# Moving a projection, two prefetches and an image load to other units of a software-pipelined Mamba block

## The chip, the cores and the metric

The kernel runs on one core of one Trainium2 chip. The metric is the device time in microseconds of one launch. The kernel before takes 27343.99 us, the median of three runs from 27331.65 to 27346.93 us. A further execution was recorded by the profiler; its own time is 27302.98 us, and the span that the profile shows is 27301.2 us.

The engines have the names that the profile uses. PE is the matrix engine, and PEld its weight load. DVE is the vector engine, ACT the scalar engine (activation functions and copies), POOL the GpSimd engine. SP only issues DMA transfers here. Each engine carries out its own list of instructions in order and waits on semaphores for the others.

## The reference

The input is a batch of 8 images with 64 channels and 128 x 128 pixels, all in float32. The first layer reads every image as sequences of 128 pixels, once along its rows and once along its columns. Each sequence goes through a small Mamba block forwards and backwards, the results are averaged, normalised in four groups of channels, passed through SiLU and added to the image:

```
x, z  = split(in_w @ seq);  x = silu(causal_conv4(x) + conv_b)
dt, B, C = split(xp_w @ x); delta = softplus(dt_w @ dt + dt_b)
h_t = exp(delta_t * A) * h_{t-1} + (delta_t * x_t) * B_t      # 128 channels, 16 states
y_t = sum_states(h_t * C_t) + D * x_t;  out = out_w @ (y * silu(z))
```

The second layer is a residual block: its weights are drawn from a small parameter vector, and it computes 3 x 3 convolution, batch norm, ReLU, 3 x 3 convolution, batch norm, addition of its input, ReLU.

## The kernel before

**Chunks.** An image is cut into 32 chunks of four rows (o = 0, "row chunks") and then 32 chunks of four columns (o = 1, "column chunks"), each chunk 512 pixels. With 8 images that is 512 chunks. `PER` = 64 is the number of chunks of an image; below, a chunk is named by its number within the image, 0 to 63. For a row chunk the input is read straight from the resident image `xt` in SBUF; for a column chunk ACT first gathers its pixels into `xc` (L253).

**Units.** A chunk is worked through in 16 units, r = 0 to 15. A unit is one pair of 32-channel groups, four of the 16 states and one direction, laid out as 128 partitions x 1024 elements. The steps of a unit are:

- `decay` (L361, L364): ACT writes exp(A * delta) into one of two PSUM tiles, `dA0` for even units and `dA1` for odd ones. So decay of unit s+1 has to wait until the scan of unit s-1 has read that tile.
- `b_rows` (L353): PE spreads the B rows of two units into the PSUM tile `pb`.
- `drive` (L373): DVE multiplies `du` (delta times x) by `pb` into `s`. In the units 2, 5, 9, 12 and 15 (`GPS`) POOL does this instead, from a tile `bt` that a DMA has spread.
- `scan` (L381 forwards, L383 backwards): DVE runs the recurrence in place in `s`.
- `weigh` (L388): POOL multiplies `s` by the C rows.
- `add_up` (L404): PE folds two finished units into the output tile `yp`, four units later.

**The next chunk and the last one.** While the units of chunk n run, `prepare` takes one step per unit for chunk n+1: convolution and input projection into `cp` (L235 or L241, units 1 to 4), SiLU (unit 5), `dp` (L273, unit 6), `bp` and `bc` (L278, L283, unit 7), softplus (unit 8), `du` and `dl` and their stores to DRAM (L300, L302, L295, unit 9), the replicated loads of `dl` and `du` (L324, units 10 to 13), and `zp` with its copy `sz` (L315, unit 13). The chunk before is finished: DVE gates `yp` with `sz` in unit 3 (L411), and `emit` then projects it. PE multiplies by out_w into the PSUM tile `op` (L417); in a column chunk it also adds the row result, read transposed through an identity matmul (L422). ACT copies `op` into the image result `xp` (L430 for rows, L435 twice for columns). For a column chunk DVE then takes statistics of what was written (`bn_stats`, L439). In the kernel before these are units 12, 13 and 14.

**Shared buffers.** The PSUM tiles `cp`, `dp`, `op`, `cps` (first convolution of the second layer) and `gps` (normalisation) use one buffer, tag "pt". `pb`, `bp` and `zp` use another, tag "b". A tile can be written only when the readers of the tile before it are done. The image `xt`, the image result `xp` and two `strip` tiles exist once.

**Work per image.** When the last column chunk of an image has been projected, in chunk 0 of the next image, the statistics are combined (`normalize`). In the chunks 1 to 16, units 5 and 7, ACT normalises a part of `xp`, POOL adds the input and the sum is stored to DRAM as `x1`. The first convolution (`conv1`) reads `x1` back in strips: `strip_of` issues two or more DMAs per strip, and the matmuls (L494) start in unit 14 of chunk 6, three steps of two matmuls and a copy per chunk. Its first two strips are issued by the first call of the generator, `next(conv3, None)`. The next image is loaded into `xt` in chunk 62.

**The order** is written out by hand: the main loop runs over the units and calls these steps, and every engine gets its instructions in that order. All the DMAs named here are issued by SP, in one list with the waits that the program put in front of each of them; an issue that waits holds up the ones behind it. The rest of the kernel, the second convolution and the last pass, follows the loop and is not touched.

Of the kernel before, what the change touches and what calls it, by code (L numbers as in the profile page):

```python
# [17 lines left out]
W = 128  # L18
HH = W // 2
# [13 lines left out]
def tile_mamba2d_then_resblock(ctx: ExitStack, tc: tile.TileContext, x, par, gn, p_w, o_w, new_p, bn, cst, out):  # L33
    nc = tc.nc
    B = x.shape[0]
# [30 lines left out]
    with tc.tile_pool(name="prep", bufs=2) as prep, tc.tile_pool(name="prep_ps", bufs=2, space=PSUM) as prep_ps:  # L66
# [4 lines left out]
        for o, p in enumerate(par):  # L71
# [10 lines left out]
            for hf in range(2):  # L82
                h = slice(hf * C, (hf + 1) * C)
# [72 lines left out]
        for k, w in enumerate((w1, w2s)):  # L156
            nc.vector.memset(w, 0.0)
            for blk in range(2):
                for e in range(2):
                    for m in range(2):  # L160
                        kh = 2 * blk - e - m + 1
                        if 0 <= kh < 3:
                            nc.sync.dma_start(
                                out=w[e * C : (e + 1) * C, blk, :, m * C : (m + 1) * C],
                                in_=wacc[k * C : (k + 1) * C, 3 * kh : 3 * kh + 3, :],
# [37 lines left out]
    with ExitStack() as st:  # L203
# [9 lines left out]
        xt = big.tile([P, HH, W], F32, name="xt")  # L213
# [6 lines left out]
        zeros = big.tile([P, 2, SEQ], F32, name="zeros")  # L220
        nc.vector.memset(zeros, 0.0)

        def load_image(b):
            xb = x[b].rearrange("p (h w) -> p h w", w=W)
            RB = HH // 8
            for k in range(8):
                nc.sync.dma_start(out=xt[:, k * RB : (k + 1) * RB, :], in_=xb[:, k * RB : (k + 1) * RB, :])

        def project(ps, lhsT, g, s, start, stop):

# [103 lines left out]
        def c_rows(g, r):  # L334

            half, ng, d = where(r)
            t = rep.tile([P, N], F32, name="c", bufs=5)
            src = g["bd"][NS + 4 * ng : NS + 4 * ng + 4, d, :]
            nc.sync.dma_start(out=t, in_=src.partition_broadcast(32))
            g["c", ng, d] = t  # L340

        def b_tile(g, r):

            half, ng, d = where(r)
            t = rep.tile([P, N], F32, name="bt", bufs=3)
            nc.sync.dma_start(out=t, in_=g["bd"][4 * ng : 4 * ng + 4, d, :].partition_broadcast(32))
            g["bt", r] = t

        def b_rows(g, r):

            half, ng, d = where(r)
            pb = psa.tile([P, N], F32, name="pb", tag="b")
            nc.tensor.matmul(pb, wt[g["o"]]["wb"][:, P * ng : P * (ng + 1)], g["u"][:, d, :], start=True, stop=True)  # L353
            g["pb"] = pb

        def decay(g, r):

            half, ng, d = where(r)
            dA = g["dA", r] = psa.tile([P, 2, SEQ, W], F32, name=f"dA{half}")
            t, edge = (slice(1, W), 0) if d == 0 else (slice(0, W - 1), W - 1)  # L360
            nc.scalar.copy(dA[:, :, :, edge], zeros)  # L361
            dl = g["dl", half, d].rearrange("p q (s t) -> p q s t", t=W)
            for j in range(2):
                nc.scalar.activation(  # L364
                    dA[:, j, :, t], dl[:, j, :, t], AF.Exp, scale=wt[g["o"]]["A"][:, 2 * half + j, ng : ng + 1]
                )

        def drive(g, r):

            half, ng, d = where(r)  # L370
            s = unit.tile([P, 2, N], F32, name="s")
            engine, b = (nc.gpsimd, g.pop(("bt", r))) if r in GPS else (nc.vector, g["pb"])
            engine.tensor_mul(s, g["du", half, d], b.unsqueeze(1).to_broadcast([P, 2, N]))  # L373
            g["s", r] = s
# [10 lines left out]
        def weigh(g, r):  # L385
            half, ng, d = where(r)
            s, c = g["s", r], g["c", ng, d]
            nc.gpsimd.tensor_mul(s, s, c.unsqueeze(1).to_broadcast([P, 2, N]))  # L388
# [123 lines left out]
        PER = 2 * NCH  # L512
# [2 lines left out]


        PREP = range(14)
        OUT = 12
        NORM = (5, 7)
        CONV = (14, 15, 0, 1, 2)  # L520
        gs = [dict(b=b, o=o, i=i) for b in range(B) for o in range(2) for i in range(NCH)]
        total = UN * len(gs)
        stats = {}
        pieces, norm, conv3, output = (iter(()) for _ in range(4))

        def at(s):
            return gs[s // UN], s % UN

        def fetch(s):

            for k in range(10):
                r = (s + k) % UN
                if 0 <= s + k < total and r in GPS and k == {GPS[0]: 9, GPS[1]: 4}.get(r, 7):
                    b_tile(*at(s + k))
                if 0 <= s + k < total and r % 2 == 0 and k == {0: 7, 4: 4}.get(r, 5):
                    c_rows(*at(s + k))

        def ahead(r):

            return 2 if r == GPS[0] else 3  # L540

        with tc.manual_schedule():
            load_image(0)
            for _ in prepare(gs[0], None):
                pass
            for s in range(-9, 0):
                fetch(s)
            decay(*at(0))
            b_rows(*at(0))
            drive(*at(0))  # L550
            for s in range(total + UN):
                n, r = divmod(s, UN)
                live = n < len(gs)
                prev = gs[n - 1] if n else None
                if r == 0:
                    for _ in pieces:
                        pass
                    pieces = prepare(gs[n + 1], gs[n]) if n + 1 < len(gs) else iter(())
                if s + 1 < total:
                    decay(*at(s + 1))  # L560
                    if (s + 1) % UN not in GPS:
                        drive(*at(s + 1))
                for k in (2, 3):
                    if s + k < total and (s + k) % UN in GPS and ahead((s + k) % UN) == k:
                        drive(*at(s + k))
                if live:
                    scan(*at(s))
                    weigh(*at(s))
                if r == LAG - 1 and prev:
                    gate(prev)  # L570
                if s == total - 1:
                    nc.scalar.activation(gs[n]["sz"], gs[n]["sz"], AF.Silu)
                if s % 2 == 0 and s + 2 < total:
                    b_rows(*at(s + 2))
                if r in CONV and n % PER > 6 or r >= CONV[0] and n % PER == 6:
                    next(conv3, None)
                if r in PREP:
                    next(pieces, None)
                if r == LAG and live:
                    skip(gs[n])  # L580
                if s % 2 == 0 and LAG <= s < total + LAG:
                    add_up(*at(s - LAG))
                if r in NORM and n % PER:
                    next(norm, None)
                fetch(s)
                if r == OUT and prev:
                    if n % PER == 6:
                        next(conv3, None)
                    output = emit(prev)
                    next(output)  # L590
                elif r == OUT + 1:
                    next(output, None)
                elif r == OUT + 2:
                    next(output, None)
                    if n % PER == 0 and prev:
                        for _ in conv3:
                            pass
                        norm = normalize(prev["b"], stats.pop(prev["b"]))
                        next(norm)
                        conv3 = conv1(prev["b"])  # L600
                elif r == 8 and live and n % PER == PER - 2 and gs[n]["b"] + 1 < B:
                    load_image(gs[n]["b"] + 1)

            for _ in range(2 * 5):
                next(norm)
            next(conv3)
            for _ in range(NT):
                for _ in range(2):
                    next(norm, None)
                for _ in range(5):  # L610
                    next(conv3)


    with ExitStack() as st:
# [15 lines left out]
        mean, r = pooled(small, [pps[:, 0:1], pps[:, 1:2]], mv, bmat, "bn1")  # L630
# [8 lines left out]
        st2 = small.tile([P, B, NT, 6], F32, name="st2")  # L639
        RB = HH // 4  # L640
        for b in range(B):
            xp = xps[b % 2]
            cb = c1_d[b].rearrange("p (h w) -> p h w", w=W)
            for k in range(0, HH + 1, RB):
                ct = stage.tile([P, RB, W], F32, name="ct")
                for e in range(2):
                    es = slice(e * C, (e + 1) * C)
                    lo, hi = max(k, e), min(k + RB, HH + e)
                    if lo < hi:
# [5 lines left out]
                if 0 < k < HH:  # L655
                    nc.scalar.activation(xp[:, k : k + RB, 1 : W + 1], ct, AF.Relu, bias=t, scale=s)
            c2v = c2_d[b].rearrange("(v c) (j e w) -> v c j e w", c=C, e=2, w=W)
            for k in range(0, NT, 2):
                ps = psw.tile([P, 2, N], F32, name="cps")
                for j in range(2):  # L660
                    for kw in range(3):
                        for blk in range(2):
                            r = SEQ * (k + j) + blk
# [10 lines left out]
                for e in range(2):  # L674
                    nc.sync.dma_start(
                        out=c2v[hf, :, j0 : j0 + 2 * SEQ, e, :],
                        in_=cs[e * C : (e + 1) * C].rearrange("p (j w) -> p j w", w=W),
# [4 lines left out]
        mean, r = pooled(small, [pps[:, 2:3], pps[:, 3:4]], mv2, bmat, "bn2")  # L682
# [72 lines left out]
```

## Time and profile before

| | value |
|---|---|
| median of three runs | 27343.99 us |
| profiled execution, its own time | 27302.98 us |
| its span | 27301.2 us |
| DVE busy | 25670.1 us, 94% |
| POOL busy | 25128.9 us, 92% |
| PE busy | 19712.4 us, 72% |
| ACT busy | 18444.1 us, 68% |
| one DVE scan (L381, L383) | 2.28 us, 8192 of them |
| one DVE drive (L373) | 1.20 us, 5632 of them |
| one POOL operation (L388, L373) | 2.36 and 2.37 us, 8192 and 2560 of them |
| granted PE clock, mean | 0.857 of full speed |
| DMA traffic | 4871.19 MB, 178 GB/s |

In a line of the waits view stand the engine and line that waited, what it waited for, the sum in us, how often, and the longest. In a line of the timeline stand the start and the duration in us, the engine, the line of the kernel, the operation, the tiles that it writes and reads, the shape, and how many instructions were merged; in brackets is the idle time of the engine before it and what ended it. A line of the windows view gives a stretch in us from the start of the span, its length, the busy time of the five engines in it with the number of instructions, the granted PE clock, the share of DMA time and the rate.

Where several semaphores are waited for, the profile names the one that came last by its records; an engine that had been done long before is then not the cause.

### The profile page before, as it was taken

To read this page: it belongs to the slowest core of one execution; us is meant where nothing else is said; L and a number is where in the kernel's file an instruction comes from. 1 tells how busy PE (TensorE), PEld (TensorE's weight loads), DVE (VectorE), ACT (ScalarE), POOL (GpSimd) and SP (SyncE) were. 2 spreads that over 40 slices of the span, in tenths; PEclk is the share of its full clock that TensorE was granted. 3 is DMA by queue.
4 is the path that set the end of the run, shared out by engine and by line. 5 is a ranking of instruction groups with operands and counts; after the bars stand their busy time and mean duration, and the time that the engine had idled before them with its cause. 6 is when DMAs were issued, how large, how long until landed. Compare 5 with 4: busy or idle time off the path is not lost.

```text
span 27301.2 us, 235600 instructions
## 1 busy us (share of the span) xinstructions
PE 19712.4 (72%) x65580; PEld 6768.1 (25%) x65580; DVE 25670.1 (94%) x15633; ACT 18444.1 (68%) x31150; POOL 25128.9 (92%) x10916
## 2 busy tenths in 40 slices
PE   6777777777777777777677777777777777777776
PEld 1222222222222222222222222222222222222232
DVE  8999999999999999999999999999999999999942
ACT  5776667676677766767667666676676766667632
POOL 7999999999999999999999999999999999999930
PEclk8888888888888889888888888888888888888888
DMA  5555555555555455555555555555555555555545
GB/s 180 177 173 172 181 186 183 175 170 181 194 179 173 170 184 194 179 171 170 186 193 176 172 174 186 188 176 173 175 189 184 173 175 178 190 181 171 177 139 188
DMA packets 2165563, 4871.19 MB, mean 178 GB/s; under 512 B 265856, under 2 KB 413456, under 8 KB 2148368
## 3 DMA queue, kind: packets, MB, share of 16 engines
q1 hardware_dynamic: 2143648, 4754.51, 51.6%
q10 hardware_dynamic: 15984, 68.06, 0.9%
q0 software_dynamic: 4608, 33.56, 0.3%
q8 instruction: 517, 8.47, 0.1%
q14 instruction: 806, 6.60, 0.1%
HBM read 4115.52 MB, written 738.98 MB: 178 GB/s over the span
## 4 chain that ended last, share of the span: by engine, by line
DVE 35%; PE 25%; issue 21%; ACT 9%; DMA 7%; SPq 2%; POOL 1%; DVEq 0%; POOLq 0%; ACTq 0%
DVE s L373 14%; DVE s L383 10%; DVE s L381 8%; PE pb L353 7%; PE yp L404 6%; DMA du<-dd 5%; ACT dA L364 4%; PE cps L664 2%; PE dp L273 2%; DVE du L300 2%; PE cp L241 2%; PE op L417 1%; DVE y L411 1%; PE op L422 1%; PE bp L278 1%
## 5 line engine op out<-in xcount | busy, mean ns | idle before, releaser
L388 POOL TENSOR_TENSOR s<-s,c 128x1024 f32<-128x1024 f32 x8192 | 19135.7, 2363 | 887.2 <-DVE s L383 596.3
L364 ACT ACTIVATE dA<-dl,A 128x508 f32<-128x508 f32 x16384 | 11275.4, 688 | 534.8 <-DMA dl<-dd 18.0
L353 PE MATMUL pb<-u,wb 128*128 128x512 f32 x8192 | 5589.3, 770 | 7026.0 <-DVE s L373 6298.3
L383 DVE TENSOR_TENSOR_SCAN s<-dA,s 128x1024 f32<-128x1024 f32 x4096 | 9301.2, 2281 | 51.6 <-ACT dA L364 43.1
L381 DVE TENSOR_TENSOR_SCAN s<-dA,s 128x1024 f32<-128x1024 f32 x4096 | 9296.8, 2280 | 0.0
L373 DVE TENSOR_TENSOR s<-du,pb 128x1024 f32<-128x1024 f32 x5632 | 6776.9, 1203 | 269.9 <-PE pb L353 156.5
L373 POOL TENSOR_TENSOR s<-du,bt 128x1024 f32<-128x1024 f32 x2560 | 6066.2, 2370 | 207.3 <-DMA bt<-bd 154.9
L404 PE MATMUL yp<-s,fold 128*32 128x512 f32 x32768 | 5386.0, 736 | 2.8 <-POOL s L388 2.8
L361 ACT COPY dA<-zeros 128x8 f32<-128x8 f32 x8192 | 1375.8, 168 | 5700.8 <-DVE s L383 3245.0
L353 PEld LDWEIGHTS pb<-u,wb 128*128 128x128 f32 x8192 | 1523.5, 223 | 10331.1 <-DVE s L373 5159.3
L241 PE MATMUL cp<-xc,wc 128*128 128x256 f32 (+3 forms) x8192 | 2190.9, 414 | 0.0
L235 PE MATMUL cp<-xt,wc 128*128 128x512 f32 (+3 forms) x4096 | 2033.1, 620 | 127.3 <-DMA xt<-x_h 75.9
L241 PEld LDWEIGHTS cp<-xc,wc 128*128 128x128 f32 x8192 | 1676.7, 211 | 1074.4 <-issue 461.2
L404 PEld LDWEIGHTS yp<-s,fold 128*32 128x32 f32 x32768 | 699.9, 117 | 3863.7 <-POOL s L388 2139.0
L364 ACT ACT_TABLE_LOAD x1030 | 1321.5, 1283 | 26.5 <-DMA dl<-dd 8.4
L315 ACT COPY sz<-zp 128x512 f32<-128x512 f32 x512 | 300.1, 586 | 1331.1 <-PE zp L241 852.1
L235 PEld LDWEIGHTS cp<-xt,wc 128*128 128x128 f32 x4096 | 770.6, 199 | 1433.5 <-issue 1071.4
L273 PE MATMUL dp<-u,wd 128*128 128x512 f32 x2048 | 978.6, 601 | 1.2 <-ACT u L266 1.2
L394 PE MATMUL yp<-u,dg 128*128 128x512 f32 x2048 | 961.9, 592 | 1.0 <-DVE y L411 1.0
L693 POOL DMA_DIRECT2D out<-cc x32 | 17.2, 537 | 968.7 <-ACT cc L692 968.7
L494 PE MATMUL cps<-strip,w 128*128 128x512 f32 x1536 | 750.5, 615 | 104.1 <-DMA strip<-x_d 88.1
L417 PE MATMUL op<-y,wo 128*128 128x512 f32 x1024 | 720.4, 792 | 0.8 <-DVE y L411 0.8
(109 smaller groups left out, 10513.4 us busy)
## 6 DMA issues: line engine op xcount, KB each, us to landing
dl<-dd SPq DMA_DIRECT2D x2048, 512.0 KB
du<-dd SPq DMA_DIRECT2D x2048, 512.0 KB
c<-bd SPq DMA_DIRECT2D x4096, 256.0 KB
bt<-bd SPq DMA_DIRECT2D x2560, 256.0 KB
dd<-du SPq DMA_DIRECT2D x2048, 128.0 KB
dd<-dl SPq DMA_DIRECT2D x2048, 128.0 KB
bd<-bc SPq DMA_DIRECT2D x512, 128.0 KB
c_d<-cs SPq DMA_DIRECT2D x256, 256.0 KB
```

Of the source, the lines that this page charges most:

```text
L235: nc.tensor.matmul(ps[:, :, lo:hi], lhsT[hf], xt[:, r : r + SEQ, lo - s : hi - s], start=start, stop=stop)
L241: nc.tensor.matmul(ps[:, :, lo:hi], lhsT[hf], g["xc"][:, :, lo - s - hf * HH : hi - s - hf * HH], start=start and hf == 0, stop=stop and h ...
L273: nc.tensor.matmul(dp[:, d, :], w["wd"], u[:, d, :], start=True, stop=True)
L353: nc.tensor.matmul(pb, wt[g["o"]]["wb"][:, P * ng : P * (ng + 1)], g["u"][:, d, :], start=True, stop=True)
L361: nc.scalar.copy(dA[:, :, :, edge], zeros)
L364: nc.scalar.activation(dA[:, j, :, t], dl[:, j, :, t], AF.Exp, scale=wt[g["o"]]["A"][:, 2 * half + j, ng : ng + 1])
L373: engine.tensor_mul(s, g["du", half, d], b.unsqueeze(1).to_broadcast([P, 2, N]))
L381: nc.vector.tensor_tensor_scan(s, a, s, 0.0, ALU.mult, ALU.add)
L383: nc.vector.tensor_tensor_scan(s[:, ::-1], a[:, ::-1], s[:, ::-1], 0.0, ALU.mult, ALU.add)
L388: nc.gpsimd.tensor_mul(s, s, c.unsqueeze(1).to_broadcast([P, 2, N]))
L404: nc.tensor.matmul(g["yp"][32 * q : 32 * (q + 1), :], fold, s[:, j, :], start=False, stop=r == UN - 2, skip_group_check=True,)
L417: nc.tensor.matmul(op, w["wo"].rearrange("p h c -> p (h c)"), g["y"], start=True, stop=o == 0)
```

## The change

`OUT` goes from 12 to 10: the projection of the chunk before is issued in unit 10, its copies in unit 11, and for a column chunk its statistics in unit 12. In the first chunk of an image the statistics of the image before and the start of its normalisation move with them. The first call of `conv3`, which issues an image's first two strips, goes from unit 12 to unit 2 of chunk 6. `load_image` issues one eighth of an image per call instead of all eight; it is called in the units 2, 4, 6 and 8 of the chunks 62 and 63 instead of once in unit 8 of chunk 62. The first image is still loaded at once ahead of the loop. The number of instructions and of DMAs and their sizes stay as they were.

```diff
-        def load_image(b):
-            xb = x[b].rearrange("p (h w) -> p h w", w=W)
-            RB = HH // 8
-            for k in range(8):
-                nc.sync.dma_start(out=xt[:, k * RB : (k + 1) * RB, :], in_=xb[:, k * RB : (k + 1) * RB, :])
+        def load_image(b, k):
+
+            rows = slice(k * (HH // 8), (k + 1) * (HH // 8))
+            nc.sync.dma_start(out=xt[:, rows, :], in_=x[b].rearrange("p (h w) -> p h w", w=W)[:, rows, :])
...
-        OUT = 12
+        OUT = 10
         NORM = (5, 7)
         CONV = (14, 15, 0, 1, 2)
+        LOAD = (2, 4, 6, 8)
...
-            load_image(0)
+            for k in range(8):
+                load_image(0, k)
...
                 fetch(s)
+                if r == CONV[-1] and n % PER == 6:
+                    next(conv3, None)
+                if r in LOAD and live and n % PER >= PER - 2 and gs[n]["b"] + 1 < B:
+                    load_image(gs[n]["b"] + 1, LOAD.index(r) + 4 * (n % 2))
                 if r == OUT and prev:
-                    if n % PER == 6:
-                        next(conv3, None)
                     output = emit(prev)
                     next(output)
...
-                elif r == 8 and live and n % PER == PER - 2 and gs[n]["b"] + 1 < B:
-                    load_image(gs[n]["b"] + 1)
```

## The prediction

> **What bounds the kernel now.** I read the page's busy shares first, then the table of waits, then four consecutive chunks cut out by windows, then the timeline of one chunk.
>
> ```profile
> PE 19712.4 (72%) x65580; PEld 6768.1 (25%) x65580; DVE 25670.1 (94%) x15633; ACT 18444.1 (68%) x31150; POOL 25128.9 (92%) x10916
> ```
>
> DVE is busy 94% of the span, POOL 92%, and the slices show that most of what DVE lacks lies in the last two of forty, where the second convolution runs. In the main loop DVE is the bound with POOL close behind. A saving must therefore be DVE idle time in the loop:
>
> ```profile
> DVE gst L439 <- ACT xp L435: 329.3, 191, 5.1
> ...
> DVE s L373 <- PE pb L353: 156.5, 237, 8.0
> ...
> DVE s L373 <- DMA du<-dd: 103.7, 93, 11.6
> ...
> PE cps L494 <- DMA strip<-x_d: 88.1, 13, 28.5
> ```
>
> (Columns: total, times, longest, us.) The statistics of a column chunk wait for ACT's copies 191 times; about 590 us of idle on DVE is what any reordering here can reach. Four column chunks, from first scan to first scan:
>
> ```profile
> 5697.27:5749.86 52.59, 38.95 (x132) 14.97 (x132) 49.78 (x32) 35.85 (x62) 48.73 (x22) 0.81 0.52 179
> 5749.86:5799.36 49.50, 34.99 (x132) 13.73 (x132) 49.49 (x31) 35.86 (x62) 48.73 (x22) 0.89 0.46 159
> 5799.36:5850.80 51.44, 37.81 (x132) 14.53 (x132) 49.78 (x31) 35.85 (x62) 48.78 (x22) 0.83 0.51 173
> 5850.80:5902.07 51.27, 37.63 (x132) 14.47 (x132) 49.78 (x31) 35.85 (x62) 48.79 (x22) 0.83 0.53 177
> ```
>
> (Length, then busy PE, PEld, DVE, ACT, POOL, granted clock.) The second has DVE busy 49.49 of 49.50: this is a column chunk's floor. The others lose 1.8 to 3.1 us, with a lower PE clock. The mean of the 248 ordinary column chunks is 51.15. The end of the fourth on PE, then on DVE:
>
> ```profile
> 5882.77 2.08 PE L353 MATMUL pb<-u,wb 128*128 128x512 f32 x2 [5.70 <-DVE s L373]
> 5884.77 1.93 PE L404 MATMUL yp<-s,fold 128*32 128x512 f32 x8
> 5888.26 2.08 PE L353 MATMUL pb<-u,wb 128*128 128x512 f32 x2 [1.56 <-DVE s L373]
> 5890.27 1.52 PE L404 MATMUL yp<-s,fold 128*32 128x512 f32 x8
> 5891.71 1.12 PE L417 MATMUL op<-y,wo 128*128 128x512 f32 x2
> 5892.68 1.88 PE L422 MATMUL op<-xp,ident 128*128 128x512 f32 x2
> 5894.37 1.04 PE L241 MATMUL zp<-xc,wz 128*128 128x256 f32 x4
> ```
> ```profile
> 5888.12 2.29 DVE L381 TENSOR_TENSOR_SCAN s<-dA,s 128x1024 f32<-128x1024 f32 x1
> ...
> 5893.71 2.27 DVE L383 TENSOR_TENSOR_SCAN s<-dA,s 128x1024 f32<-128x1024 f32 x1
> 5897.18 0.43 DVE L439 BATCH_NORM_STATS2 gst<-xp 128x6 f32<-128x256 f32 x1 [1.20 <-ACT xp L435]
> ```
>
> PE does add-up (8,9), the projection, zp in one row; ACT copies sz, then xp twice; DVE has finished scan 14 at 5895.98 and waits until 5897.18. The first pb takes 2.08 us after 5.70 us of idle and 1.12 later: PE is slow after idling.
>
> [...] its clock changes on a 3.413 us grid, no slow window less than 0.81 busy was followed by a fast one, and the four chunks above sum to 204.80 us, 60 windows: the chunks have locked to that grid. [...] the xp copy behind sz (5895.94 after 5895.45, both long after op ended) agrees. [...] SP's timeline of a load chunk agrees:
>
> ```profile
> 6542.43 6.16 SPq L227 DMA_DIRECT2D xt<-x_h  x8
> 6549.48 4.02 SPq L295 DMA_DIRECT2D dd<-du  x4
> 6554.47 4.42 SPq L295 DMA_DIRECT2D dd<-dl  x4
> ```
>
> In the chunk before, each group of four stores took 1.73 and 1.81.
>
> **Projection at unit 10, copies 11, statistics 12.** Nothing is added or removed: the two column matmuls (one in row chunks), two copies (one) and one statistics instruction move two units up, and no DMA with them. Call 5882.77 zero. DVE ends scan 12 at +7.64, and the statistics now stand behind it. PE reaches the projection behind add-up (6,7): +2.00 plus 1.87 slow is +3.88. Its wait on the dp buffer is met (du and dl are read by then). Slow, op takes 1.87 and ident 1.72, ending at +7.47; fast, 0.97 and 1.70, at +6.55; if add-up is fast too, at +5.7. ACT's two copies end 1.4 later (0.19 to the first, 1.21 for both) and the statistics start 0.05 after: ident's end plus 1.45. The wait is so 1.28 with op slow, 0.36 with op fast, 0 with add-up fast. Queued behind on PE: pb for unit 14, formerly at +5.49, now after ident; ready 1.1 later, before the statistics end, so hidden by their wait. Behind on ACT: decay 13, 1.6 us, done at ident's end plus 3.0; scan 13 can start at plus 2.9. Hidden to 0.1. Later zp follows drive 14, sz follows decay 14, pb 16 is ready at about +12.7 plus the wait, drive 16 asks at +13.5 plus the wait: 0.8 spare.
>
> When does the clock come back? PE is now busy from 0 through pb, add-up, projection, so the first full window turns it fast between +2.95 and +6.36 by phase. Wait as a function of that time t: 0.48t-1.51, at most 1.28. A chunk of 49.5 plus its wait is 14.5 windows plus the wait, which moves the phase on; followed by hand this visits about 0.80, 1.23, 1.27, 0.03 in turn, mean 0.83. Unit 3's wait for pb, untouched, stays (0.16 per chunk now; I take 0.10). So 50.43, against 51.15: 0.72 x 248 = **179 us**. Ends: 0 if the phase sticks at 51.2 (15 windows), 370 if almost no wait is left.
>
> Row chunks: DVE's idle sorted by position has 81 us ahead of drive 16, in chunks where a slow op pushed zp, sz and pb 16 back. With op gone from unit 12 pb 16 has over 1 us to spare. But 42 us of it lie in the chunks 1 to 17 of an image, where POOL (21 operations at 2.33, one of 1.27 for the residual) needs 50.2 of their 50.3 us, so little is kept: **40** of 81 (ends 0 and 81). The seven chunks that close an image's statistics: the same 0.7 each, **5**.
>
> **First strips in unit 2 of chunk 6.** Four DMAs and a 0.17 us memset move ten units ahead, past SP's bd, dd stores, the residual's load and store, some c and bt and six of the eight copies dl/du. Before, the first convolution matmul waits:
>
> ```profile
> 3721.72 3.75 PE L494 MATMUL cps<-strip,w 128*128 128x512 f32 x4 [8.91 <-ACT dA L364]
> ```
>
> ACT had long been done; SP issued the strips at 3709.35 to 3713.81. Behind it stands pb, and DVE waits 7.9 us for that. Chunk 7 averages 58.7 where its neighbours take 50.5; the last rows they read are stored in chunk 5, unit 7, so at unit 2 nothing holds them and they have 12 units, some 37 us. 7 x 8.2 = 57; I take **55**. The cover is the slack of c and bt fetches, asked four to nine units ahead; if gone, a microsecond or two each.
>
> **Image loads in eighths.** Eight DMAs of 512 KB leave one burst for units 2, 4, 6, 8 of two chunks. Chunk 62 averages 57.4 against 51.2: 6.2 x 7 = 43. Each eighth has two units (6 us) before the next and precedes the stores of unit 9; I leave 0.5 us per chunk of residue and add the projection's 0.7 in chunk 62: **41** (ends 0 and 48). The first eighth waits for ACT's read of xt at unit 0, behind it only fetches with slack.
>
> **Sum.** 179+40+5+55+41 = 320. The profiled execution took 27303 (span 27301.2 and 1.8 around it), so 26983. The median of the runs is 41 above the profiled one: **27025**.
>
> **Rivals.** (1) The column chunks stay at 15 windows: 51.2 is a fixed point if waits in a chunk can reach 1.7. My largest is 1.28 plus 0.39 in unit 3, not at the same phase; 0.3 us later on PE would do it. Gain 141: 27205. (2) The projection is mostly fast: I have PE's phase walk wrong and the mean wait is 0.3. Gain 450: 26895. (3) Slower: ACT now waits for op at unit 11 with decay 13 behind. If POOL lags, add-up (6,7) is late, op with it, and DVE waits for statistics and decay. Now weigh 7 ends about 7 us before add-up needs it. To eat all other gains the wait must be above 2.1 us per chunk, which needs weigh 7 some 9 us later, four POOL operations. POOL is busy 48.8 of the new 50.4, so it still catches up. Place: PE ahead of op. At 2.5 us per chunk: 49.5 + 2.5 + 0.1 is 52.1, 236 more and 141 less than before, 27440. (4) The load and strip moves are hidden anyway or collide with c: gain 96 less, 27120; the DVE waits of 7.9 and 3.4 us speak against it.
>
> **Chances.** Forecast (26950 to 27110) 0.55, rival 1 0.19, rival 2 0.09, rival 4 0.08, rival 3 or an unseen wait 0.09. The range from 26925 to 27215 takes in the forecast and rivals 1 and 4 and leaves out 2 and 3, 0.18. A change of 0.2% (55 us) is what a measurement here can tell from none. Faster 0.89, same 0.03, slower 0.08.
>
> **What would show it.** Waits: statistics on ACT from 329 to about 210 us, the convolution's strip wait from 88 to near 30 (the last image's stays), du on DMA to about 60; chunk 7 at 50.5, chunk 62 near 50.6, column chunks mixing 49.5 and 50.8. Wrong if column chunks sit at 51.2, if drive 14 waits for pb, or if scan 13 waits for decay.

## The result and the profile after

The changed kernel takes 27036.85 us (median of five runs, 27023.71 to 27060.69), against 27335.58 us for the kernel before (here five runs too, 27329.18 to 27346.93): 299 us less, a ratio of 0.9892 with a 95% interval of 0.9877 to 0.9906. The forecast was 27025.

The profiled execution of the kernel after took 27036.85 us, the same as its median, while that of the kernel before lay below its median. From profile to profile the gain is only 266 us (spans 27301.2 and 27035.1), and it is this difference that can be taken apart. The lines of the functions below `load_image` have moved up by one in the kernel after, so L439 is now L438 and L373 is L372.

The engines' busy shares of the kernel after, from the head of its page:

```profile
PE 19433.8 (72%) x65580; PEld 6667.4 (25%) x65580; DVE 25638.5 (95%) x15633; ACT 18477.9 (68%) x31150; POOL 25139.5 (93%) x10916
```

The instruction counts are those of before. PE's busy time fell by 279 us with the same 65580 matmuls: by the clock record 53471 of them started at the full clock, where it was 51453, and the mean granted clock rose from 0.857 to 0.878. The waits of the kernel after that answer to those shown of before (who waited for what, us in total, times, longest):

```profile
DVE gst L438 <- ACT xp L434: 225.0, 209, 4.1
...
DVE s L372 <- DMA du<-dd: 88.4, 124, 11.4
...
PE cps L493 <- DMA strip<-x_d: 41.1, 7, 27.8
DVE s L372 <- PE pb L352: 32.6, 94, 1.5
```

The statistics still wait 225 us, where it was 329. The wait for pb is down to a fifth. The wait for du only fell from 104 to 88, although the image loads no longer cause any of it: it has grown somewhere else. Five column chunks of the kernel after, cut from first scan to first scan (length, then busy PE, PEld, DVE, ACT, POOL, then PE's clock, DMA share and rate):

```profile
5337.50:5388.47 50.97, 37.52 (x132) 13.96 (x132) 49.65 (x32) 35.93 (x62) 48.78 (x22) 0.87 0.49 168
5388.47:5439.35 50.88, 37.57 (x132) 13.94 (x132) 49.55 (x31) 35.92 (x62) 48.76 (x22) 0.87 0.54 183
5439.35:5490.23 50.88, 37.28 (x132) 13.78 (x132) 49.55 (x31) 35.92 (x62) 48.76 (x22) 0.87 0.51 175
5490.23:5539.89 49.66, 34.69 (x132) 13.32 (x132) 49.55 (x32) 35.95 (x62) 48.77 (x22) 0.88 0.50 168
5539.89:5590.27 50.38, 36.30 (x132) 14.18 (x132) 49.58 (x31) 35.93 (x62) 48.81 (x22) 0.87 0.52 184
```

Chunks with waits of about 1.3 us still follow on each other, then come one with almost none and one with a middle one. The wait goes with the phase of PE's clock, whose record changes here too only on a grid of 3.413 us (one step of it is called a window). In the 232 ordinary column chunks in which a column chunk is projected, the statistics wait at most 0.23 us where the clock turns full less than 3.5 us after the first pb, and 1.26 to 1.34 us where it does so after more than 5.5. The end of one of the slow kind, first on PE, then on DVE:

```profile
5672.86 2.08 PE L352 MATMUL pb<-u,wb 128*128 128x512 f32 x2 [5.70 <-DVE s L372]
5674.87 1.94 PE L403 MATMUL yp<-s,fold 128*32 128x512 f32 x8
5676.73 2.05 PE L416 MATMUL op<-y,wo 128*128 128x512 f32 x2
5678.60 1.90 PE L421 MATMUL op<-xp,ident 128*128 128x512 f32 x2
5680.32 1.04 PE L352 MATMUL pb<-u,wb 128*128 128x512 f32 x2
```
```profile
5678.22 2.28 DVE L380 TENSOR_TENSOR_SCAN s<-dA,s 128x1024 f32<-128x1024 f32 x1
5681.77 0.43 DVE L438 BATCH_NORM_STATS2 gst<-xp 128x6 f32<-128x256 f32 x1 [1.27 <-ACT xp L434]
5682.12 1.20 DVE L372 TENSOR_TENSOR s<-du,pb 128x1024 f32<-128x1024 f32 x1
```

pb, add-up and the first matmul of the projection (L416) now run one after the other at half clock; the clock record of this trace turns to full at 5678.63, as the identity matmul (L421) starts. pb for unit 14 starts only at 5680.32, 7.46 us after the first pb, and the statistics wait 1.27 us. Drive 14 stands behind them on DVE: its pb ends at 5681.36, the statistics start at 5681.77 and drive 14 at 5682.12.

Sorted by kind of chunk, with the mean distance of first scans in microseconds in the profiles of before and after:

| chunks | number | before | after | gain in all |
|---|---|---|---|---|
| ordinary column chunks, 32 to 61 | 240 | 51.15 | 50.51 | 154 |
| row chunks 1 to 5, 8 to 17 | 120 | 50.33 | 50.28 | 6 |
| row chunks 18 to 31 | 112 | 49.82 | 49.74 | 9 |
| chunks 6 and 7 | 16 | 54.06 | 50.17 | 62 |
| chunks 62 and 63 | 15 | 53.98 | 50.57 | 51 |
| chunk 0, where an image's statistics are closed | 7 | 55.63 | 56.45 | -6 |

These sum to 276, 10 more than the difference of the spans; the loop's ends hold the rest.

### The profile page after: what moved, and what is told of

Same layout as the page of the kernel before. It is cut to its first block, busy times and chain, and to the rows that moved or that the text cites. A ratio compares the mean times of both kernels' runs of the same rounds, so it can differ in the third digit from the quotient of the medians.

```text
span 27035.1 us, 235698 instructions
## 1 busy us (share of the span) xinstructions
PE 19433.8 (72%) x65580; PEld 6667.4 (25%) x65580; DVE 25638.5 (95%) x15633; ACT 18477.9 (68%) x31150; POOL 25139.5 (93%) x10916
## 4 chain that ended last, share of the span: by engine, by line
DVE 35%; PE 22%; issue 18%; ACT 12%; DMA 9%; SPq 2%; POOL 1%; DVEq 0%; POOLq 0%; ACTq 0%
DVE s L372 15%; DVE s L382 9%; DVE s L380 8%; DMA du<-dd 7%; PE pb L352 6%; ACT dA L363 6%; PE yp L403 5%; PE cps L665 2%; PE dp L272 2%; DVE du L299 2%; PE op L421 1%; PE op L416 1%; DVE y L410 1%; PE bp L277 1%; ACT xp L434 1%
## 5 line engine op out<-in xcount | busy, mean ns | idle before, releaser
L352 PE MATMUL pb<-u,wb 128*128 128x512 f32 x8192 | 5455.4, 753 | 6516.4 <-DVE s L372 5728.6
L372 DVE TENSOR_TENSOR s<-du,pb 128x1024 f32<-128x1024 f32 x5632 | 6742.2, 1197 | 132.7 <-DMA du<-dd 88.4
L372 POOL TENSOR_TENSOR s<-du,bt 128x1024 f32<-128x1024 f32 x2560 | 6071.0, 2371 | 149.6 <-DMA bt<-bd 147.3
L403 PE MATMUL yp<-s,fold 128*32 128x512 f32 x32768 | 5196.3, 712 | 5.2 <-POOL s L387 5.2
L240 PE MATMUL cp<-xc,wc 128*128 128x256 f32 (+3 forms) x8192 | 2068.0, 397 | 0.0
L240 PEld LDWEIGHTS cp<-xc,wc 128*128 128x128 f32 x8192 | 1585.9, 199 | 1029.5 <-issue 459.6
L434 ACT COPY xp<-op 64x256 f32<-64x256 f32 x512 | 317.5, 620 | 887.6 <-PE op L421 884.6
L416 PE MATMUL op<-y,wo 128*128 128x512 f32 x1024 | 821.8, 895 | 0.9 <-DVE y L410 0.9
```

What stands on the lines that cost most here:

```text
L240: nc.tensor.matmul(ps[:, :, lo:hi], lhsT[hf], g["xc"][:, :, lo - s - hf * HH : hi - s - hf * HH], start=start and hf == 0, stop=stop and h ...
L403: nc.tensor.matmul(g["yp"][32 * q : 32 * (q + 1), :], fold, s[:, j, :], start=False, stop=r == UN - 2, skip_group_check=True,)
L416: nc.tensor.matmul(op, w["wo"].rearrange("p h c -> p (h c)"), g["y"], start=True, stop=o == 0)
```

## The experiments

Ten kernels were run. Three take single parts of the change, one moves the projection by one unit, one keeps PE busy, two follow a wait that was not expected, and three combine these. They ran on three chips, each group beside runs of the kernel before, whose medians were 27326.57, 27334.44 and 27341.40 us; gains below are against the median of the same group, where the kernel after stands at 299.

**The projection alone.**

```diff
-        OUT = 12
+        OUT = 10
...
+                if r == 12 and prev and n % PER == 6:
+                    next(conv3, None)
                 if r == OUT and prev:
-                    if n % PER == 6:
-                        next(conv3, None)
...
-                elif r == 8 and live and n % PER == PER - 2 and gs[n]["b"] + 1 < B:
+                if r == 8 and live and n % PER == PER - 2 and gs[n]["b"] + 1 < B:
```

The load stays at unit 8 of chunk 62.

> Only the projection moves (units 10, 11, 12); strips and loads stay as before. Theory (PE's place in unit 12 and its slow clock set the column chunks' wait): column chunks go from 51.15 to about 50.5, 248 of them, so 160 us less than before, near 27175; DVE's wait for the statistics falls from 329 to about 215 us and stands behind scan 12; the waits of chunk 7 (60 us on pb) and of chunk 62 (40 us on du) stay. Rival (strips and loads carry the gain): within 40 us of before.

Measured: 27142.51 us, 184 less than before, ratio 0.9931 (0.9919 to 0.9943). The statistics wait 225.3 us, where it is 225.0 in the kernel after, and the mean clock is 0.878 as after. The waits of chunk 7 for pb (59 us) and of chunk 62 for du stay. So this part carries three fifths of the gain, and the rival falls.

**The strips alone.**

```diff
+                if r == CONV[-1] and n % PER == 6:
+                    next(conv3, None)
                 if r == OUT and prev:
-                    if n % PER == 6:
-                        next(conv3, None)
```

> Only the first strips move to unit 2 of chunk 6. Theory: the convolution's matmul no longer waits for its strip, chunk 7 goes from 57.8 (mean of eight) to 50.4, 55 to 60 us less than before, near 27278; everything else as before. Rival (the wait is given back in the chunks after, because POOL is then the bound): under 20 us less.

Measured: 27264.54 us, 62 less than before, ratio 0.9978 (0.9970 to 0.9986). Chunk 7 went from 57.75 to 50.6, and DVE's wait for pb in it from 60 to 3 us. On PE the convolution's wait for its strips is

```profile
PE cps L494 <- DMA strip<-x_d: 44.7, 9, 28.4
```

and all nine of these waits lie behind the loop, for the last image, which the change leaves alone. The rival falls: chunks 8 to 17 of the eight images became only 4 us longer in all.

**The image loads alone.** `OUT` and the first call of `conv3` are those of before, `load_image` and its calls those of after.

> Only the image loads are split over chunks 62 and 63. Theory: DVE's wait for du in chunk 62 (3.4 to 11 us each, 40 us in all) goes, chunk 62 goes from 57.4 to 51.3, 40 to 45 us less than before, near 27293. Rival (the eighths collide with the fetches of c and bt and only spread the wait): under 15 us less, with waits on du, c or bt in chunks 62 and 63.

Measured: 27291.76 us, 35 less than before, ratio 0.9988 (0.9982 to 0.9995). In chunks 62 and 63 DVE's wait for du went from 39.6 us to 0.9. The three single parts sum to 281 us, against 299 for all of them together: they act at different places and nearly add.

**The projection in unit 11.**

```diff
-        OUT = 10
+        OUT = 11
```

> The kernel after with the projection in unit 11, copies 12, statistics 13. PE's order is the same as with unit 10, since PE gets nothing else in unit 11, and the statistics have one more scan of slack. Theory (what is left is PE: projection in front of pb for unit 14, at half clock): the wait moves from the statistics to drive 14 on pb, 0 to 1.05 us a chunk, mean 0.65; column chunks about 50.3, 40 us less than after, near 27000. Rival (what is left is the statistics standing too early on DVE): the wait goes, column chunks 49.6 to 49.7, 200 to 220 us less than after, near 26825.

Measured: 26906.14 us, 420 less than before, ratio 0.9846 (0.9833 to 0.9859), so 122 less than the kernel after. This lies between the 40 of the theory and the 200 to 220 of the rival. No wait for the statistics is left in the column chunks; the waits of DVE are now

```profile
DVE s L372 <- PE pb L352: 143.1, 268, 0.9
...
DVE s L372 <- DMA du<-dd: 97.6, 125, 12.0
```

and 115 us of the first line lie in the ordinary column chunks, 106 of them in front of drive 14, 0.46 us a chunk. The wait moved to pb, as the theory said, but it is smaller than the 0.65 expected, and the column chunks came to 50.07. PE's list is the same in both kernels; in the kernel after the wait stands in front of the statistics, 0.84 us a chunk, and moving these behind scan 13 took away about half of it. Again the chunks fall into a pattern on the clock's grid, here of three:

```profile
5467.05:5517.46 50.41, 35.92 (x132) 13.84 (x132) 49.51 (x32) 36.02 (x62) 48.82 (x22) 0.87 0.50 171
5517.46:5566.85 49.39, 35.16 (x132) 13.59 (x132) 49.39 (x32) 36.01 (x62) 48.71 (x22) 0.88 0.51 175
5566.85:5617.20 50.35, 36.74 (x132) 14.48 (x132) 49.62 (x31) 36.00 (x62) 48.84 (x22) 0.87 0.53 182
```

150.15 us are 44 windows of 3.413.

**PE kept busy.** Sixteen matmuls by zeros follow add-up (4,5) in unit 8 when a column chunk is to be projected.

```diff
+        def fill(g, count):
+
+            for k in range(count):
+                q = 32 * (k % 4)
+                nc.tensor.matmul(
+                    g["yp"][q : q + 8, :], zeros.rearrange("p j q -> p (j q)"), g["u"][:, 0, :],
+                    start=False, stop=False, skip_group_check=True,
+                )
...
                     add_up(*at(s - LAG))
+                if r == 8 and live and prev and prev["o"] == 1:
+                    fill(gs[n], 16)
```

> The kernel after, with sixteen matmuls by zeros (8 columns, 512 rows, added to the output tile, which they leave as it is) on PE behind add-up (4,5) in unit 8, whenever the chunk to be projected is a column chunk; 4.2 us of PE work at full clock in its idle stretch of 5.7 us. Theory (PE's half clock after that stretch sets the wait): the first pb of the stretch's end takes 1.1 us instead of 2.1, the projection ends by +5.7, the statistics' wait of 225 us falls under 40, column chunks 49.6, 200 to 230 us less than after, near 26820, although PE has 1 ms more work. Rival (the wait is the projection's length and position, not the clock): PE's work grows, no gain, 27030 to 27100; or the fillers run at half clock (7.7 us) and push pb 12 back by 2 us, slower.

Measured: 26852.86 us, 482 less than before, ratio 0.9823 (0.9810 to 0.9837), so 183 less than the kernel after, with 8160 matmul instructions more; 200 to 230 had been expected. PE at the same place as above:

```profile
5537.08 3.62 PE L412 MATMUL yp<-u,zeros 128*8 128x512 f32 x32
5542.97 1.12 PE L352 MATMUL pb<-u,wb 128*128 128x512 f32 x2 [2.27 <-DVE s L372]
5544.02 1.07 PE L403 MATMUL yp<-s,fold 128*32 128x512 f32 x8
5545.02 1.13 PE L425 MATMUL op<-y,wo 128*128 128x512 f32 x2
5545.98 1.87 PE L430 MATMUL op<-xp,ident 128*128 128x512 f32 x2
5548.46 1.13 PE L352 MATMUL pb<-u,wb 128*128 128x512 f32 x2 [0.61 <-DVE s L372]
```

The idle stretch is 2.27 us instead of 5.70, the first pb takes 1.12 instead of 2.08, and pb for unit 14 waits for DVE again. In the kernels before and after, the first pb at this place takes more than 1.5 us in every column chunk; here it does in 34 of 247. The identity matmul gives way to pb by 6.37 us after the first pb at the latest, where it was 7.47. The statistics wait 24.3 us instead of 225, and column chunks are 49.77. That the half clock after an idle stretch sets the wait is shown: the only thing added is work. Part of the gain went to another wait: that of DVE for du in ordinary column chunks rose from 7 to 27 us.

**du ahead of dl.**

```diff
-            for k, what in enumerate(("dl", "du")):
+            for k, what in ((1, "du"), (0, "dl")):
```

> The kernel after, with du issued ahead of dl in each of the four replicated loads. Theory (in row chunks DVE's drive 16 now waits for du's transfer, 54 us in chunks 8 to 31 and 14 in chunks 1 to 6): du comes about 0.6 us sooner, dl has slack on ACT until scan 16, the wait on du falls to about 25 us, 30 to 40 us less than after, near 27000. Rival (both land together, or ACT's decay becomes the late one): within 15 us of after, with more waits of scans on ACT.

Measured: 26930.56 us, 404 less than before, ratio 0.9852 (0.9838 to 0.9865), so 105 less than the kernel after, three times what was expected. The waits of DVE:

```profile
DVE s L372 <- PE pb L352: 32.1, 89, 0.7
...
DVE s L372 <- DMA du<-dd: 14.1, 6, 7.9
```

du had cost 54 us in row chunks 8 to 31 and 14 in chunks 1 to 6; 2 and 0.3 are left. What remains lies at the start of the loop. ACT itself now waits 64 us for dl, but scans wait 42 us for ACT in both kernels, so dl had the slack. Row chunks 8 to 31 together became 72 us shorter, chunks 1 to 6 17 us; DVE's idle time accounts for 58 and 14 of that, and the rest is not assigned. (The profile also puts 114 us of waits of POOL's weigh in the kernel after down to du, here 18 to du and 42 to dl. Weigh reads neither, so these names are not used.)

The issue of du moved up by about 0.6 us; the waits of more than a microsecond that vanish need more. The landings can be read from the semaphore updates in the traces, for the first pair of a chunk in row chunks 8 to 31. In the kernel after, dl lands 6.73 us after its issue and du, issued 0.59 us behind it, 7.85 us after its own: du lands 1.72 us behind dl. With the order swapped it is du that lands 6.77 us after its issue, and dl comes 1.59 us behind it. In the other pairs of a chunk the second lands about 1.3 us behind the first, in either order. So the two transfers of 512 KB land one behind the other, in the order of their issue, and du is now the first. It lands 6.08 us ahead of the chunk's first scan instead of 4.70.

**du ahead of dl in the kernel before.** The same edit.

> The kernel before with du issued ahead of dl. In its row chunks drive 16 waits 40 us for pb and 28 us for du in chunks 8 to 31; in the kernel after it is 10 and 54. Theory (two waits stand behind one another there, and taking away one lets the other show): the wait on du goes nearly to nothing, but the wait on pb grows by 10 to 25 us, and the gain, 106 us in the kernel after, is only 50 to 75 us here, near 27270. Rival (the two waits fall in different chunks): the wait on pb stays at 40 and the gain is that of the du waits, chunk 62 included, 85 to 105 us, near 27240.

Measured: 27256.53 us, 85 less than before, ratio 0.9971 (0.9959 to 0.9982). The wait on pb grew to

```profile
DVE s L373 <- PE pb L353: 175.2, 272, 9.2
...
DVE s L373 <- DMA du<-dd: 38.3, 14, 7.8
```

from 156.5, by 13 us in row chunks 8 to 31 (40.1 to 53.3) and 11 in ordinary column chunks, while it fell by 7 in chunks 1 to 6, and the wait on du in row chunks went to 1.2. So part of each wait had covered the other, as the theory said; but the total lies at the edge that the rival named, and 26 us of du's wait stayed in chunk 62. The two were not cleanly told apart by the total: profile to profile the gain is 62 us, between medians 85.

**Combinations.**

> Fillers as in the run with the filled PE, and the projection in unit 11. Theory: with PE at full clock pb for unit 14 is ready at +6.7, before drive 14 asks at +7.6, so neither place waits and this is within 30 us of the filled PE with unit 10, near 26810. Rival (clock is not what is left): as unit 11 without fillers, near 26906, or above it.

Fillers and unit 11: 26803.68 us, 531 less than before, ratio 0.9806 (0.9792 to 0.9819), 49 less than with fillers and unit 10. A difference of up to 30 was expected. Unit 11 still helps by taking the remaining 24 us of statistics and shortening chunk 0 from 56.6 to 54.9.

> The kernel after with the projection in unit 11 and du ahead of dl, without fillers. The one takes 130 us from column chunks, the other 106 us mainly from row chunks: if they add, 26800; the fillers then are worth 125 us more in the version that has all three (26674). Rival (in column chunks du's wait was hidden by the others and its gain shrinks): 26830 or more.

Unit 11 and du first, without fillers: 26814.84 us, 527 less than before, ratio 0.9807 (0.9793 to 0.9820). The two single gains over the kernel after, 122 and 105, sum to 227; measured are 228. The rival falls.

> Both of the last and du ahead of dl: the waits are at different places, so the gains add: 30 to 40 us less than with fillers and unit 11, near 26775. Rival: POOL (49.0 of 49.5 us a chunk) takes the place of the waits that go, within 15 us of fillers and unit 11.

All three: 26674.47 us, 660 less than before, ratio 0.9758 (0.9745 to 0.9771), and 361 less than the kernel after. This is the best version found. Putting du first is worth 129 us here where 30 to 40 were expected, as DVE's wait for du fell from 119 us with fillers and unit 11 to 14. So the rival, that POOL takes the waits' place, falls. The fillers are worth 133 us here (660 against 527), where 125 were expected. They do not hold the clock everywhere: the first pb takes more than 1.5 us in 112 of 247 column chunks. The ordinary column chunks are 49.50 and the row chunks 24 to 31, which have no convolution, 49.14.

## Why the prediction was right, step by step

The forecast of 27025 was met within 12 us, partly by luck: my sum of 320 us was made against the profiled execution, and there the gain is 266, 54 less. Against that stood the 41 us that I added because the profile of before lay below its median; the profile of after did not. The two errors nearly cancelled. The signs and places were right for the three large parts; two small steps were wrong.

**Projection, column chunks: 179 expected, 154 to 159 measured.** The working held to hundredths. (A time with a plus counts in us from the first pb, as in the prediction.) That a busy window brings the full clock is shown by the traces: in the first 26 ms of before and after, a window at half clock that was followed by one at full clock was at least 0.81 busy on PE (2071 cases), and one followed by another at half clock at most 0.87. A window at full clock that was followed by one at half was at most 0.51 busy. In the 232 chunks the clock turned full between +2.96 and +6.30, where +2.95 to +6.36 was expected. With op at half clock the identity matmul was to end at +7.47; in the chunk shown it ends at +7.46, and over the column chunks the end lies between +6.11 and +7.47, mean 7.02, where the mean wait of 0.83 plus 6.19 asks for 7.02. The wait itself is 0.84 in the mean of the ordinary column chunks. The statistics' wait was expected to be about 210 us and was 225. The mean chunk is 50.51 instead of 50.43, so the 248 chunks of the prediction give 159, and the 240 of the table 154. The order of phases was not quite the one walked by hand: most often waits of about 0.8, 1.0, 1.3 and 1.3 us come before one of none, a cycle of five chunks instead of four.

**Row chunks: 40 expected, about 15 measured.** The step that failed is the reading of the 81 us in front of drive 16 as all due to a slow projection that pushes zp and pb 16 back. In the profile of before only half of them are waits for pb: in the row chunks 1 to 5 and 8 to 31 it is 39 us for pb and 39 for du. After, it is 0 for pb, as forecast, and 67 for du; with the projection alone 0 and 58. Drive 16 needs both, and where pb no longer ended the wait, du did. The profile names one releaser per wait, the last one, and the second was nearly as late. Over all places in row chunks 8 to 31, DVE's wait for pb fell from 40.1 to 10.1 us and that for du rose from 27.9 to 53.6. And POOL was not the floor that I took it for: with du first, chunks 1 to 17 average 49.89, below the 50.2 that I reckoned from 2.33 us an operation.

**Closing chunks: 5 expected, minus 6 measured.** Chunk 0 became 0.8 us longer. DVE's waits in it are the same in sum, 2.9 and 2.8 us: that for the statistics' copies shrank from 1.2 to 0.5, but 0.6 for pb 16 came up. What grew is one instruction of the normalisation that moved with the projection, a subtraction of 128 x 1 elements on DVE, from 0.27 us in the mean of these chunks to 1.17. One of the long ones, and what POOL did:

```profile
9821.71 2.34 POOL L387 TENSOR_TENSOR s<-s,c 128x1024 f32<-128x1024 f32 x1
...
9822.41 1.65 DVE L176 TENSOR_TENSOR d_gn<-gmv,m_gn 128x1 f32<-128x1 f32 x1
```

In the traces of before and after it takes 0.16 us in the eight places where POOL stands idle beside it, and 0.37 to 1.70 in the eight where POOL runs. In all twelve profiles, wherever it takes more than 0.3 us, it ends 0.01 to 0.02 us after an instruction of POOL ends. With the projection in unit 11 it takes 0.21 us, and chunk 0 is 55.4. So the instruction seems to be held up by POOL, and where it falls relative to POOL's operations decides its length. No run changed this alone. The forecast had no such term.

**Strips: 55 expected, 59 to 62 measured** in the trace and alone. **Loads: 41 expected**; chunks 62 and 63 became 51 shorter, of which the projection accounts for some 9 by estimate (0.64 us a chunk), and alone the loads gave 35 by the medians and 38 in the chunks 62 and 63 of the trace. That SP's stores came out more slowly behind the burst is measured (each four in 4.02 and 4.42 us against 1.73 and 1.81 in the chunk before); by what means the burst slowed them was not shown. Of the signs named, the wait for du missed: 88 us against about 60, by what it gained in the row chunks.

**Rivals.** The lock at 15 windows (rival 1) would have left column chunks at 51.2; they are 50.5, but the chunks of 50.97 show how near it is. The mostly fast projection (rival 2) is what PE with fillers shows, where the mean wait is below 0.1. POOL's lag (rival 3) did not come: scan 13 does not wait for its decay. Strips and loads that bring nothing (rival 4) are refuted by the two single runs.

## What to carry to other kernels

When an engine's wait follows the half clock of PE, lay the instructions out in time for both clocks: which of them occurred here went with the idle stretch ahead (behind 5.70 us the first pb took 2.08 us, behind 2.27 us it took 1.12), and filling that stretch brought more than moving the work by a unit again (183 us against 122). Where one instruction needs two inputs, the wait in the profile names the later one only (in row chunks 8 to 31 the wait for pb fell by 30 us and that for du rose by 26); before counting it as gain, ask when the other is ready. Issue the transfer that is needed first also first, even when both are issued within a microsecond (0.59 us apart here).

## What was not expected

The length of a chunk takes the grid of PE's clock: four chunks before made 204.80 us, 60 windows of 3.413, and three with unit 11 made 150.15, 44 windows. This is no accident of the stretches shown. Taken to 0.05 us, about half of all stretches of four ordinary column chunks before (110 of 216) are 60 windows, and with unit 11 and du first all 200 stretches of three are 44. With fillers in unit 10 no stretch of one to seven chunks shows such a pattern, but with all three parts four fifths of the pairs are 29 windows, so 49.50 is 14.5 of them. The wait goes with the clock's phase, and a longer chunk moves that phase in turn; my reading is that chunks so linger where waits are long: in the kernel after, 87 of the 232 wait 1.26 to 1.34 us and 40 less than 0.1.

The identity matmul of the projection, whose moving operand is read with a stride of 512 bytes, takes 1.70 us at the full clock from its start to that of the next instruction, while the one before it, of the same shape, takes 0.97. It seems hardly to depend on the clock: where up to 0.6 us of it fall under the half clock, it takes 1.73 (63 cases in the trace of before). It almost never ran wholly at half clock; in the profile of before one pair did, and its second half started 0.86 us after its first, as with part of it at half clock.

Swapping the issue of two transfers of 512 KB, 0.6 us apart on SP, in each of the four loads of a chunk took 105 us from the kernel after.
